# A hybrid block on one core: the first group's two batches as units of their own up to the first expert layer

## The chip, the core and the metric

One core of a Trainium2 chip runs the whole block as one program. Its engines are TensorE (PE, and PEld for its weight loads), VectorE (DVE), ScalarE (ACT), GpSimd (POOL) and the DMA queues, of which SP, ACT and POOL issue here. The metric is the device time of one execution in microseconds; lower is better.

## What is computed

The input is 8 batches of 256 tokens with 128 features, float32. Four layers follow one another, each on a layer-normalised input and added back to it: a state space layer, an expert layer, an attention layer, and the same expert layer again.

```python
x = x + state_space(layernorm(x))
x = x + experts(layernorm(x))
x = x + attention(layernorm(x))
x = x + experts(layernorm(x))
```

The state space layer normalises again, projects to a hidden part and a gate part of 256 channels each, runs a causal convolution of 4 taps and silu over the hidden part, derives from it delta (256 channels, through softplus) and the rows B and C (16 each), and then runs a recurrence over the tokens for every channel and each of 16 states:

```python
new = exp(A * d_t) * state + d_t * B_t * h_t
y = sum_n(new * C_t) + D * h_t      # then times silu(gate), then the output projection
```

The expert layer has 8 experts of width 352. A router gives each token its two best experts and their shares; every expert is computed for every token (gate, up, down) and weighted with its share, which is zero for all but two. Attention uses squared relu instead of softmax, and multiplies by u.

## The kernel before

The 8 batches are worked on as four groups of two, so a tile is 128 channels by 512 tokens. A group goes through these pieces, each a Python generator that gives out one operation at a time:

- `prelude` (s): statistics and row normalisation, transposition to channels by tokens, the hidden projection (`hid`), the convolution (for group 0 on DVE, L561 and L563; for groups 1 and 2 on PE, `conv`), the projection `xpj`, from which the B and C rows go to DRAM (`bc`, L585), and `dt` with softplus on ACT and DVE (L596 to L633), which gives `dl` (delta) and `du` (delta times h).
- `feeder`: loads the B and C rows of some states, spread over all partitions (`bt`, `ct`, L682, issued by SP), and computes the decays exp(A delta) on ACT (L697). There are three decay tiles in rotation.
- `recurrence` (m): on DVE, for each chunk of states and each of two channel halves, three instructions of 128x1024: multiply by `bt` (L744), scan (L749), multiply by `ct` (L753). A tile of 1024 holds 2 states of 2 batches. There are 16 such triples per group. All but some of the results are added up by accumulating DMAs that POOL issues (`adder`, L716).
- `gating` (g): the gate projection and silu. `ending` (f): for groups 0 and 1 PE sums the states of the last tiles by multiplying with the identity (`y`), and DVE multiplies with the gate (L797). `tail` (t): the output projection and its addition to x (`pb_m`, L512).
- `rest` (r): `led_in` (layer norm, transposition `tp_p`, the router's logits `lg_p`, ranks and shares on DVE, L895 to L921, and the first expert's weighting, L940), `moe` (22 slices of gate `gp_p`, up `up_p`, down `dn_p`, with silu on ACT, L960, and the product `it_p` on DVE, L1000), attention, a second `led_in`, and a second `moe` (tiles ending in `_r`).

`led_in`, the end of `moe` and attention already know parts of a group (`PARTS`): a group in `SPLIT` has one part per batch. `SPLIT` is empty before, so every group is one part.

The order on the engines is made while the program is built. `Board` keeps for each engine the time at which it comes free in a plan, with a cost for each operation (`mm`, `act_us`, `dve_us`). At each step it asks every lane for its next operation, takes the earliest possible start, and among the lanes of that engine that can start then, the lowest rank (`RANKS`, one number for each piece and group; `feeder` and `adder` have one each). Where ACT has to change its function table, the plan adds 1.3 us to the operation, and to the comparison only where the operation became possible less than `LONG` ago. Where PE would be idle before an operation that begins a new PSUM tile, the plan fills the gap with matmuls of the identity by itself into that tile, one for each 0.23 us (`Board.do`; the matmul stands at L325). The fillers are ordinary instructions of PE's list.

```python
            idle = t - max([self.free.get(op.engine, 0.0)] + [h.used for h in op.out])
            for _ in range(int((idle - 0.3) / self.FILL)):
                op.fill()
```

Of the kernel before, what the change touches and what calls it, by code (L numbers as in the profile page):

```python
# [31 lines left out]
class Board:  # L32
# [4 lines left out]
    PATIENCE, LONG = 0, 0  # L37
# [58 lines left out]
def kernel(  # L96
# [27 lines left out]
    nc = tc.nc  # L124
# [26 lines left out]
        "s": [0, 4, 4, 1.5], "m": [1.5, 2, 3, 3.5],  # L151
        "g": [4, 0, 3.5, 2], "t": [0, 3.5, 3.5, 0.5],
        "r": [2, 0.5, 2.5, 0.5], "f": [2.5, 1.5, 4, 0.5], "w": [0, 0, 0.3, 0], "feeder": 5, "adder": 0,
    }
    SOON = ("p0", "p1", "r0", "p3", "r3")
    SPLIT = ()
# [125 lines left out]
    def ring(pool, shape, tag, name, bufs=1):  # L282

        held = rings.setdefault((pool.name, tag), [])
        free = held[-bufs].used if len(held) >= bufs else 0.0
        h = Held(pool.tile(shape, FP, tag=tag, name=name, bufs=bufs), free)
        held.append(h)
        return h
# [91 lines left out]
    ]  # L380
    xh = [
# [4 lines left out]
    padding = [Held(t) for t in padded]  # L386
# [131 lines left out]
    def prelude(g):  # L518

        GB = SIZES[g]  # L520
        G = GB * T
        xn = yield from layernorm(Held(xs[g]), f"m{g}", "m", rms=True, parts=xh[g])
        for held in xh[g]:
            yield from biased(held, b_first)
        xT = ring(norm, [P, G], "xTm", f"xT_m{g}")
        yield from transposed(xn, f"m{g}", xT, scale=col("norm_scale"))

        h = [ring(mam, [P, G], f"h{c}", f"h_{g}_{c}", bufs=2) for c in range(NI)]  # L530
        cv = ring(mam, [P, NI, GB, T], "ex", f"cv_{g}")
        for c in range(NI):
            hp = padding[c]
            ps = bank([P, G], f"hid_{g}_{c}")
            yield pe(mm(G), [ps], [xT], product(ps.ap, [(in_w_sb[:, c * P : (c + 1) * P], xT.ap)]))
            yield act(act_us(G), [hp], [ps], lambda: nc.scalar.activation(
                hp.ap[:, 0:GB, K - 1 :], ps.ap.rearrange("p (b t) -> p b t", b=GB),
                AF.Identity, bias=col("in_b", c),
            ))
            shut(ps)  # L540

            if g in CONV:
                cps = bank([P, GB, T], f"conv_{g}_{c}")
                yield pe(K * mm(G), [cps], [hp], product(
                    cps.ap, [(taps_sb[:, k, c, :], hp.ap[:, 0:GB, k : k + T]) for k in range(K)]
                ))
                yield act(act_us(G), [h[c]], [cps], lambda: nc.scalar.activation(
                    h[c].ap.rearrange("p (b t) -> p b t", b=GB), cps.ap, AF.Silu,
                    bias=col("conv_b", c),
                ), SILU)  # L550
                shut(cps)
                continue

            if g > 0:
                yield act(act_us(G), [cv], [hp], lambda: nc.scalar.mul(
                    cv.ap[:, c], hp.ap[:, 0:GB, 0:T], col("conv_w", c)
                ))

            def taps():
                if g == 0:  # L560
                    nc.vector.tensor_scalar_mul(cv.ap[:, c], hp.ap[:, 0:GB, 0:T], col("conv_w", c))  # L561
                for k in range(1, K):
                    nc.vector.scalar_tensor_tensor(  # L563
                        cv.ap[:, c], hp.ap[:, 0:GB, k : k + T], col("conv_w", k * NI + c),
                        cv.ap[:, c], ALU.mult, ALU.add,
                    )

            yield dve((K - (g > 0)) * dve_us(G), [cv], [hp], taps)
        for c in range(0 if g in CONV else NI):
            yield act(act_us(G), [h[c]], [cv], lambda: nc.scalar.activation(  # L570
                h[c].ap, cv.ap[:, c].rearrange("p b t -> p (b t)"), AF.Silu, bias=col("conv_b", c)
            ), SILU)


        ps = bank([P, G], f"xpj_{g}")
# [4 lines left out]
        ww = ring(mam, [P, NI, G], "ww", f"ww_{g}")  # L580
# [3 lines left out]
        bc = Held(dram.tile([2 * N, G], FP, tag="bc", name=f"bc_{g}"))  # L584
# [4 lines left out]
        dl = [ring(mam, [P, G], f"dl{c}", f"dl_{g}_{c}", bufs=2) for c in range(NI)]  # L589
        ex = ring(mam, [P, NI, G], "ex", f"ex_{g}")  # L590
        for c in range(NI):
            ps = bank([P, G], f"dt_{g}_{c}")
# [19 lines left out]
        du = [ring(mam, [P, G], f"du{c}", f"du_{g}_{c}", bufs=2) for c in range(NI)]  # L612
# [29 lines left out]
        led_up[g] = bc, h, xT, dl, du  # L642

    def gating(g):

        xT = led_up[g][2]
        G = SIZES[g] * T
        gate = [ring(mam, [P, G], f"g{c}", f"g_{g}_{c}") for c in range(NI)]
        for c in range(NI):
            ps = bank([P, G], f"gat_{g}_{c}")  # L650
            w0 = I + c * P
            yield pe(mm(G), [ps], [xT], product(ps.ap, [(in_w_sb[:, w0 : w0 + P], xT.ap)]))
            yield act(act_us(G), [gate[c]], [ps], lambda: nc.scalar.activation(
                gate[c].ap, ps.ap, AF.Silu, bias=col("in_b", NI + c)
            ), SILU)
            shut(ps)
        gates[g] = gate
# [8 lines left out]
    def feeder():  # L666

        for g in range(NG):
            while f"s{g}" not in done:
                yield None  # L670
            GB = SIZES[g]
            G = GB * T
            NC = CHUNK // GB
            bc, h, _, delta, du = led_up[g]
            for q in range(N // NC):
# [4 lines left out]
                for tag, r0 in (("bt", q * NC), ("ct", N + q * NC)):  # L680
                    t = ring(scan, [P, NC, G], tag, f"{tag}_{g}_{q}", bufs=2)
# [5 lines left out]
                fed[g, q] = *rows_at, das  # L687
                for c in range(NI):
# [15 lines left out]
                    yield act(0.81 * NC, [da], [delta[c]], issue, EXP)  # L704
# [4 lines left out]
    def adder():  # L709

        while len(done & {f"f{g}" for g in range(NG)}) < NG:
# [3 lines left out]
            g, us, acc, st, into, of = sums.pop(0)  # L715
# [4 lines left out]
            landed[g] = landed.get(g, 0) + 1  # L720
# [3 lines left out]
    def recurrence(g):  # L724
        GB = SIZES[g]
# [3 lines left out]
        bc, h, _, delta, du = led_up[g]  # L729
# [4 lines left out]
        for q in range(NQ):  # L734
            for c in range(NI):
                while not spare():
                    yield None
                st = state([P, NC, G], f"st_{g}_{q}_{c}")
                if q == 0:
                    acc.append(st)  # L740
                while len(fed.get((g, q), [[]])[-1]) <= c:
                    yield None
                bt, ct, das = fed[g, q]
# [13 lines left out]
                elif q > 0:  # L757
                    sums.append((g, 6.3, acc[c], st, acc[c].ap, st.ap))
                    count[c] += 1
                elif g > 0:  # L760

                    sums.append((g, 4.5, acc[c], h[c], acc[c].ap[:, 0, :], h[c].ap))
                    count[c] += 1
        recurred[g] = acc, last, sum(count)
# [5 lines left out]
    def ending(g):  # L770

        G = SIZES[g] * T
        NC = CHUNK // SIZES[g]
        acc, last, count = recurred.pop(g)
        bc, h, _, delta, du = led_up[g]
        if g in FOLD:
            for c in range(NI):
                sums.append((g, 4.5, acc[c], acc[c], acc[c].ap[:, 0, :], acc[c].ap[:, 1, :]))
                count += 1
        while landed.get(g, 0) < count or g not in gates:  # L780
            yield None
        for c in range(NI):
            if g in FOLD:
                yield dve(dve_us(G), [du[c]], [gates[g][c], acc[c]], lambda: nc.vector.tensor_mul(
                    du[c].ap, acc[c].ap[:, 0, :], gates[g][c].ap
# [3 lines left out]
            y = bank([P, G], f"y_{g}_{c}")  # L789
# [7 lines left out]
            yield dve(dve_us(G), [du[c]], [gates[g][c], y], lambda: nc.vector.tensor_mul(  # L797
                du[c].ap, y.ap, gates[g][c].ap
# [3 lines left out]
    def tail(g):  # L802
        gates.pop(g)
        bc, h, _, delta, du = led_up.pop(g)
        G = SIZES[g] * T
        yield from forked((RANKS["t"][g], g), [
            project_back(
                xh[g][p], of_part(g, p, du), out_w_sb, f"m{g}{p}"
            ) for p in range(len(PARTS[g]))
        ])  # L810
# [407 lines left out]
    def rest(g):  # L1218
# [15 lines left out]
        yield from forked((RANKS["r"][g], g), [led_in(g, "p", key, p, first) for p in parts])  # L1234
# [5 lines left out]
    for g in range(NG):  # L1240
        waiting.append(Lane((RANKS["s"][g], g), prelude(g), [f"g{g - 1}"] * (g > 0) + [f"t{g - 2}"] * (g > 1)))
        waiting[-1].name = f"s{g}"
        waiting.append(Lane((RANKS["m"][g], g), recurrence(g), [f"s{g}"] + [f"m{g - 1}"] * (g > 0)))
        waiting[-1].name = f"m{g}"
        waiting.append(Lane((RANKS["g"][g], g), gating(g), [f"s{g}"] + [f"t{g - 1}"] * (g > 0)))
        waiting[-1].name = f"g{g}"
        waiting.append(Lane((RANKS["f"][g], g), ending(g), [f"m{g}"]))
        waiting[-1].name = f"f{g}"
        waiting[-1].patience = RANKS["w"][g]
        waiting.append(Lane((RANKS["t"][g], g), tail(g), [f"f{g}", f"g{g}"] + [f"t{g - 1}"] * (g > 0)))  # L1250
        waiting[-1].name = f"t{g}"
        waiting.append(Lane((RANKS["r"][g], g), rest(g), [f"t{g}"] + [f"r{g - 2}"] * (g > 1)))
        waiting[-1].name = f"r{g}"
# [57 lines left out]
```

## Time and profile before

Three runs gave 758.62, 758.63 and 759.3 us, median 758.63. The profiled execution took 758.34 us.

| What | Value |
|---|---|
| profiled execution | 758.34 us |
| its span (first to last instruction) | 756.6 us |
| granted PE clock, mean | 0.999 |
| DVE, recurrence: multiply, scan, multiply | 1.23, 2.31, 1.22 us each, 64 of each |
| first multiply of the recurrence on DVE | at 39.66 us |
| first expert layer, first gate matmul | at 153.44 us |
| table loads on ACT | 89 of 1.28 us, and one at the start |
| DMA, mean | 117 GB/s |

How to read such a page: part 1 gives each engine's busy time, its share of the span and its instructions. A matmul of this kernel is recorded as two halves, so 428 recorded fillers are 214 matmuls. The chain that ended last follows from the last instruction back to what released it; its shares say which engine set the end. A row of the groups has line, engine, operation, the tile written and the tiles read, shape, count, then busy time, mean of one in ns, and the idle time before it with what ended most of it. Names are without their numbers: `y` stands for all tiles of that name. In the window tables the first columns are the window, its length, then PE, PEld, DVE, ACT and POOL busy with the count of instructions, the granted clock, the DMA share and GB/s.

### The profile page before, as it was taken

The numbers are of one execution on the slowest core, as the hardware profiler recorded it, in microseconds if no ns is written. First come the engines' busy times: TensorE is split into PE (matmuls) and PEld (weight loads), VectorE is DVE, ScalarE is ACT, GpSimd is POOL, SyncE is SP. The second block draws the span as 40 slices with busy tenths as digits, with TensorE's granted clock in tenths as the row PEclk, the third lists the DMA queues.
The fourth block names the chain that finished last, engine by engine and source line by source line (L and its number), as shares of the span: only waits on it lengthen the run. The fifth ranks groups of instructions, "written<-read, shape, count | busy, mean of one in ns | idle before, by whom it ended". The sixth has DMA issues, their size and how long they took to land.

```text
span 756.6 us, 8464 instructions
## 1 busy us (share of the span) xinstructions
PE 737.7 (98%) x3093; PEld 403.6 (53%) x3093; DVE 568.6 (75%) x824; ACT 431.1 (57%) x570; POOL 89.8 (12%) x110
## 2 busy tenths in 40 slices
PE   4999999999999999999999999999999999999997
PEld 3877996853446744434754533443555434644343
DVE  2599999999999999899999998995735334354332
ACT  5578333799947879977876677742252322432220
POOL 2021110311112210002120110011100001000000
PEclk9999999999999999999999999999999999999999
DMA  8719795399763345655774666745011200000110
GB/s 260 209 57 220 169 219 162 98 228 218 166 171 84 76 124 133 166 133 138 176 170 96 159 161 179 160 102 109 2 42 27 72 15 14 15 29 29 47 36 14
DMA packets 38903, 88.63 MB, mean 117 GB/s; under 512 B 4339, under 2 KB 14542, under 8 KB 38862
## 3 DMA queue, kind: packets, MB, share of 16 engines
q0 software_dynamic: 9312, 30.94, 22.8%
q1 hardware_dynamic: 20624, 41.54, 17.2%
q10 hardware_dynamic: 8926, 15.61, 6.8%
q8 instruction: 24, 0.39, 0.2%
q14 instruction: 17, 0.14, 0.0%
HBM read 55.71 MB, written 1.44 MB: 76 GB/s over the span
## 4 chain that ended last, share of the span: by engine, by line
PE 78%; DVE 15%; ACT 3%; issue 2%; ACTq 0%; DVEq 0%
PE gp_r L487 10%; PE dn_r L1006 10%; PE dn_p L1006 9%; PE gp_p L487 9%; PE up_r L986 7%; PE up_p L986 7%; DVE st L749 6%; PE up_r L993 3%; DVE st L744 3%; PE up_p L993 3%; DVE st L753 2%; PE av_a L1197 2%; PE tp_p L325 1%; PE xpj L325 1%; PE v_a L1131 1%
## 5 line engine op out<-in xcount | busy, mean ns | idle before, releaser
L749 DVE TENSOR_TENSOR_SCAN st<-decay,st 128x1024 f32<-128x1024 f32 x64 | 147.8, 2309 | 2.5
L960 ACT ACTIVATE sg_r<-gp_r,zero 128x512 f32<-128x512 f32 x88 | 59.9, 687 | 109.8 <-PE gp_r L487 88.7
L57 ACT ACT_TABLE_LOAD x89 | 114.2, 1283 | 8.0 <-PE dn_r L1006 3.6
L697 ACT ACTIVATE decay<-dl,zero,a_sb 128x510 f32<-128x510 f32 x128 | 96.2, 804 | 36.9 <-DVE st L749 35.7
L1000 DVE TENSOR_TENSOR it_r<-up_r,sg_r 128x512 f32<-128x512 f32 x88 | 60.4, 687 | 66.7 <-PE up_r L986 42.3
L960 ACT ACTIVATE sg_p<-gp_p,zero 128x512 f32<-128x512 f32 x88 | 59.3, 685 | 62.5 <-PE gp_p L487 46.6
L1000 DVE TENSOR_TENSOR it_p<-up_p,sg_p 128x512 f32<-128x512 f32 x88 | 60.3, 686 | 43.4 <-PE up_p L986 29.4
L1006 PE MATMUL dn_p<-it_p,wd_sb 128*128 128x512 f32 x176 | 91.2, 605 | 0.6 <-DVE it_p L1000 0.6
L1006 PE MATMUL dn_r<-it_r,wd_sb 128*128 128x512 f32 x176 | 90.5, 603 | 0.0
L716 POOL DMA_DIRECT2D st<-st x58 | 50.4, 874 | 334.2 <-DVE st L753 303.7
L487 PE MATMUL gp_r<-xT_r,wg_sb 128*128 128x512 f32 x176 | 90.0, 597 | 0.0
L487 PE MATMUL gp_p<-xT_p,wg_sb 128*128 128x512 f32 x176 | 89.0, 594 | 0.0
L744 DVE TENSOR_TENSOR st<-bt,du 128x1024 f32<-128x1024 f32 x64 | 78.8, 1231 | 0.0
L753 DVE TENSOR_TENSOR st<-st,ct 128x1024 f32<-128x1024 f32 x64 | 78.1, 1221 | 0.7
L986 PE MATMUL up_p<-wb_p,wu_sb 128*128 128x512 f32 x128 | 65.1, 594 | 0.0
L986 PE MATMUL up_r<-wb_r,wu_sb 128*128 128x512 f32 x128 | 64.9, 592 | 0.0
L1006 PEld LDWEIGHTS dn_p<-it_p,wd_sb 128*128 128x128 f32 x176 | 31.3, 189 | 47.1 <-issue 36.3
L487 PEld LDWEIGHTS gp_r<-xT_r,wg_sb 128*128 128x128 f32 x176 | 32.6, 190 | 42.7 <-issue 37.4
L1006 PEld LDWEIGHTS dn_r<-it_r,wd_sb 128*128 128x128 f32 x176 | 31.6, 190 | 44.3 <-issue 39.5
L487 PEld LDWEIGHTS gp_p<-xT_p,wg_sb 128*128 128x128 f32 x176 | 32.8, 190 | 41.2 <-issue 36.3
L325 PEld LDWEIGHTS y<-ident 128*128 128x128 f32 x428 | 48.0, 192 | 1.2 <-PE dt L487 0.8
L325 PE MATMUL y<-ident 128*128 128x128 f32 x428 | 48.2, 275 | 0.0
(217 smaller groups left out, 853.1 us busy)
## 6 DMA issues: line engine op xcount, KB each, us to landing
st<-st POOLq DMA_DIRECT2D x54, 512.0 KB, 6.4
bt<-bc SPq DMA_DIRECT2D x32, 512.0 KB, 6.0
ct<-bc SPq DMA_DIRECT2D x32, 512.0 KB, 4.5
wb_r<-wrow_r ACTq DMA_DIRECT2D x30, 256.0 KB, 3.8
wb_p<-wrow_p ACTq DMA_DIRECT2D x29, 256.0 KB, 3.9
st<-h POOLq DMA_DIRECT2D x6, 256.0 KB, 4.9
wg_sb<-in_L_ffn_w_gate_dram SPq DMA_DIRECT2D x2, 704.0 KB, 4.7
wu_sb<-in_L_ffn_w_up_dram SPq DMA_DIRECT2D x2, 704.0 KB
```

The source lines that it names most:

```text
L57: self.load_tables(op.table)
L325: nc.tensor.matmul(ps[:, 0:n], lhsT=ident[:, 0:m], rhs=ident[:, 0:n], start=True, stop=True)
L487: nc.tensor.matmul(ps, lhsT=lhsT, rhs=rhs, start=(i == 0), stop=(i == len(terms) - 1))
L697: nc.scalar.activation(shaped[:, n, :, 1:], delta[c].ap.rearrange("p (b t) -> p b t", b=GB)[:, :, 1:], AF.Exp, bias=zero, scale=a_sb[:, c, ...
L716: yield load(us, [acc], [st], lambda: nc.gpsimd.dma_start(into, of, accum_op=ALU.add), "POOL", 0.9)
L744: yield dve(1.22, [st], [bt, du[c]], lambda: nc.vector.tensor_mul(st.ap, bt.ap, du[c].ap.unsqueeze(1).to_broadcast([P, NC, G])))
L749: yield dve(2.29, [st], [das[c]], lambda: nc.vector.tensor_tensor_scan(flat, das[c].ap.rearrange("p n t -> p (n t)"), flat, 0.0, ALU.mult, ...
L753: yield dve(1.22, [st], [ct], lambda: nc.vector.tensor_mul(st.ap, st.ap, ct.ap))
L960: yield act(act_us(G), [sg], [gp], lambda: nc.scalar.activation(sg.ap, gp.ap, AF.Silu, bias=zero), SILU)
L986: nc.tensor.matmul(ps.ap, lhsT=wu_sb[:, i * P : (i + 1) * P], rhs=wa.ap[:, cols_of], start=True, stop=True,)
L1000: yield dve(dve_us(width), [it], [ps, sg], lambda: nc.vector.tensor_mul(it.ap, ps.ap, sg.ap[:, cols_of]))
L1006: yield pe(mm(dn.ap.shape[1]), [dn], [it], lambda: nc.tensor.matmul(dn.ap, lhsT=wd_sb[:, i, :], rhs=it.ap[:, cols_of], start=(i == 0), sto ...
```

## The change

Group 0 is put into `SPLIT`, and its two batches become units (`UNITS`). Every piece of the state space layer now runs per unit: `prelude`, `gating`, `feeder`, `recurrence`, `ending` and `tail` take a unit. Groups 1 to 3 are one unit each, as before. The units of a group share their tiles: `room` gives each unit its half of the group's tile and keeps the halves' use times apart. A unit of one batch has 4 states in a tile of 1024 rather than 2 states of 2 batches, so it has 8 triples; both together have 16, as before. A decay tile then takes 4 activations of 128x255 where it took 2 of 128x510.

`rest(0)` starts after the first unit's `tail`. The second batch's `led_in` waits until its own unit's `tail` is done. Before the expert layer the two parts are joined to one again, so `moe`, attention and what follows work on 512 tokens as before.

Besides, some ranks differ (`s` of group 0, `m` of group 3, `g` of group 3, `f` of group 2, and `feeder`), and `LONG` is 1.4 in place of 0.

```diff
-    PATIENCE, LONG = 0, 0
+    PATIENCE, LONG = 0, 1.4
...
-        "s": [0, 4, 4, 1.5], "m": [1.5, 2, 3, 3.5],
-        "g": [4, 0, 3.5, 2], "t": [0, 3.5, 3.5, 0.5],
-        "r": [2, 0.5, 2.5, 0.5], "f": [2.5, 1.5, 4, 0.5], "w": [0, 0, 0.3, 0], "feeder": 5, "adder": 0,
+        "s": [1.5, 4, 4, 1.5], "m": [1.5, 2, 3, 2.5],
+        "g": [4, 0, 3.5, 0.5], "t": [0, 3.5, 3.5, 0.5],
+        "r": [2, 0.5, 2.5, 0.5], "f": [2.5, 1.5, 3.5, 0.5], "w": [0, 0, 0.3, 0], "late": 0, "feeder": 2.5, "adder": 0,
...
-    SPLIT = ()
+    SPLIT = (0,)
...
+    def room(pool, u, tag, name, both=False, bufs=1):
+
+        g, lo, hi = UNITS[u]
+        if (g, tag, name) not in rooms:
+            shape = [P, NI, SIZES[g] * T] if both else [P, SIZES[g] * T]
+            rooms[g, tag, name] = ring(pool, shape, tag, f"{name}_{g}", bufs)
+            rooms[g, tag, name].views = []
+        t = rooms[g, tag, name]
+        ap = t.ap[:, :, lo * T : hi * T] if both else t.ap[:, lo * T : hi * T]
+        h = Held(ap, t.used)
+        t.views.append(h)
+        return h
...
+    UNITS = [(g, lo, hi) for g in range(NG) for lo, hi in PARTS[g]]
+    UNITS_OF = [[u for u, unit in enumerate(UNITS) if unit[0] == g] for g in range(NG)]
...
-        bc = Held(dram.tile([2 * N, G], FP, tag="bc", name=f"bc_{g}"))
+        bc = Held(dram.tile([2 * N, G], FP, tag=f"bc{lo}{g in SPLIT}", name=f"bc_{u}"))
...
-                    yield act(0.81 * NC, [da], [delta[c]], issue, EXP)
+                    yield act((0.35 + 0.0009 * G) * NC, [da], [delta[c]], issue, EXP)
...
-        yield from forked((RANKS["r"][g], g), [led_in(g, "p", key, p, first) for p in parts])
+        def come(p):
+            while f"t{UNITS_OF[g][p]}" not in done:
+                yield None
+            yield from led_in(g, "p", key, p, first)
+
+        yield from forked((RANKS["r"][g], g), [come(p) for p in parts])
+        if len(parts) > 1:
+
+            joined = Held(xs[g])
+            joined.ready = max(h.ready for h in xh[g])
+            joined.used = max(h.used for h in xh[g])
+            PARTS[g][:], xh[g][:] = [(0, SIZES[g])], [joined]
...
+    for u, (g, lo, hi) in enumerate(UNITS):
+        prior = [v for v in UNITS_OF[g - 1]] if g > 0 else []
+        older = [v for v in UNITS_OF[g - 2]] if g > 1 else []
+        lane("s", u, g, prelude(u), [f"g{v}" for v in prior] + [f"t{v}" for v in older])
+        lane("m", u, g, recurrence(u), [f"s{u}"] + [f"m{u - 1}"] * (u > 0))
+        lane("g", u, g, gating(u), [f"s{u}"] + [f"t{v}" for v in prior])
+        lane("f", u, g, ending(u), [f"m{u}"])
+        lane("t", u, g, tail(u), [f"f{u}", f"g{u}"] + [f"t{u - 1}"] * (u > 0))
+        if lo == 0:
+            lane("r", g, g, rest(g), [f"t{u}"] + [f"r{g - 2}"] * (g > 1))
```

## The prediction

> **What bounds the kernel now.** I read the page first (engine shares, then the chain that ended last), then the chain in order of time, then the busy time by stage, and last the instructions of ACT and DVE in the opening.
>
> ```profile
> PE 737.7 (98%) x3093; PEld 403.6 (53%) x3093; DVE 568.6 (75%) x824; ACT 431.1 (57%) x570; POOL 89.8 (12%) x110
> ...
> PE 78%; DVE 15%; ACT 3%; issue 2%; ACTq 0%; DVEq 0%
> ...
> L697 ACT ACTIVATE decay<-dl,zero,a_sb 128x510 f32<-128x510 f32 x128 | 96.2, 804 | 36.9 <-DVE st L749 35.7
> ...
> L325 PE MATMUL y<-ident 128*128 128x128 f32 x428 | 48.2, 275 | 0.0
> ```
>
> PE's 98% is not all work. The last row is the planner's filler: 428 recorded halves are 214 matmuls of the identity by itself, 48.2 us, 0.225 us each. The list of PE's instructions holds 564 such fillers, some 127 us. DVE holds 15% of the chain, and the chain in order of time says where:
>
> ```profile
> 43.53 1.54 ACT xn_m L437 x4
> 45.79 3.18 DVE st L749
> ...
> 126.97 1.13 DVE st L744
> 128.76 1.83 PE pb_m L506 x14
> ...
> 193.66 2.29 DVE st L749
> 197.13 1.14 DVE st L753
> ```
>
> From 45.79 to 128 us the chain is DVE alone: the first group's state space recurrence, 16 triples (multiply, scan, multiply) at 4.79 us each. Then comes the lead-in of the first expert layer; its first gate matmul starts at 153.44 in PE's timeline. DVE carries the chain again in parts until 198; from there to the end the chain is PE. The stages:
>
> ```profile
> 0.00:40.00 40.00, 29.10 (x191) 23.63 (x192) 16.67 (x47) 22.83 (x38) 5.47 (x25) 1.00 0.76 222
> ...
> 80.00:120.00 40.00, 39.95 (x333) 37.60 (x332) 39.05 (x28) 13.46 (x18) 6.07 (x7) 1.00 0.83 198
> 120.00:153.00 33.00, 32.48 (x208) 25.24 (x207) 32.31 (x54) 19.77 (x26) 7.74 (x7) 1.00 0.43 119
> 153.00:200.00 47.00, 46.42 (x157) 20.99 (x154) 46.42 (x43) 44.53 (x52) 6.88 (x8) 1.00 0.84 203
> 200.00:500.00 300.00, 299.33 (x1102) 148.22 (x1103) 279.35 (x393) 226.30 (x284) 43.86 (x45) 1.00 0.59 143
> ```
>
> [...] DVE is full from 40 to 200 us. After that PE has 0.67 us of idle in 300, so a microsecond won or lost before 200 us reaches the end if PE's stream stays whole.
>
> **The change part by part.** Everything is made against the profiled execution, 758.34 us (span 756.6 and 1.74 around it); the median of the three runs is 758.63, 0.3 above.
>
> *PE's own ledger.* PE runs its list in order, fillers too, so I compare the lists of both programs.
> - Fillers: 564 before, 519 after; 45 x 0.225 = 10.1 us removed. Of them 35 (7.9 us) stand ahead of the first gate matmul, 10 (2.3 us) behind it.
> - Sums over the states: a unit of one batch holds 4 states per tile, where the group held 2. So the 10 matmuls of 128x512 become 36 of 128x256. In PE's timeline a 512 gate matmul steps by 0.86 us and four 256-wide av_a matmuls take 1.73, so 0.433 each: 36 x 0.433 - 10 x 0.86 = +7.0 us, all ahead of the gate.
> - The eight products of 512 that the group's hid, xpj, dt and gat steps need become sixteen of 256: 16 x 0.433 - 8 x 0.86 = 0.
> - One hid product of the third group moves from ahead of the gate to behind it: 0.86 each way.
>
> Ahead of the gate: -7.9 + 7.0 - 0.9 = -1.8 us. Behind it: -2.3 + 0.9 = -1.4 us. Together -3.1 us if PE's idle time stays as it is.
>
> *DVE and ACT in the opening.* ACT normalises both batches before it makes the 10 skip and tap tiles (about 3 us). Before, three of the four xn tiles stood behind them and the first copy of the transposed rows ran at 12.94; now the first half can run at about 12.4 and takes 0.4, not 0.69. Every step to the first scan is half as long and the second unit's runs beside it. A half DVE step is taken at 0.36 us, between half of the 0.69 row and the 0.415 of uT, which is 128x256. Step by step this puts the second triple's end at about 43 us, where it was 50.2. Of these 7 us, 1.8 go back: the next group's row statistics stood ahead of the first multiply and now stand behind the fourth scan. Split work costs DVE more small steps before the router's shares are ready: two sets of seven ranking steps (1.9 us each, estimated between the 0.19 row of 32 elements and the 0.42 of 256, against 2.37 for one whole set, +1.4), two sets of shares and differences (+1.0), halved gating products, adds and guards (+0.5), and the first unit's weighting product, now ahead (+0.4): +3.3. So the router's shares are ready -7 + 1.8 + 3.3 = -1.9 us earlier, 147.3 where it was 149.2. The gate then follows after the transposition of the shares and the convolution of the third group, which now stands wholly ahead of it: about 152.4 by this path, 151.6 by PE's ledger. PE reaches the first expert layer's last product some 2 to 3 us earlier by either. DVE's list from shares to the last it_p of that layer is the same but for 0.3 us (12 scans, 25 products of 1024, 32 of 512), so DVE neither returns nor adds anything there.
>
> *Decays, where a rule speaks against it.* A decay tile was two ACTIVATEs of 128x510 (804 ns each, two in 1.52 us) and is now four of 128x255. No row has that shape with these operands. Bounds: half of the row, 1.5 us a tile (no change), and the whole row again, 3.0 us (+1.5). The Trainium skill, "ScalarE: Activation LUTs", section "What ACT_TABLE_LOAD costs", gives an ACTIVATE a fixed 186 ns, 93 ns for each pointer operand (here bias and scale), 0.833 ns an element, and lets neighbours overlap by 93 ns. That makes 797 ns at 510, which the row's 804 bears out, and so four take 4 x 584 - 3 x 93 = 2.06 us, an estimate: +0.54 a tile, 8.6 us over 16. By the rule taken alone the split costs 8.6 us; by the trace it costs nothing while ACT waits for the scan:
>
> ```profile
> 96.61 1.52 ACT L697 ACTIVATE decay<-dl,zero,a_sb 128x510 f32<-128x510 f32 x2 [3.21 <-DVE st L749]
> ```
>
> There are 3.2 us of cover in each triple, and three decay tiles in rotation. I take +0. If the cover were gone, it would be 0.54 a triple. The cover is thinnest from 43 to 90 us, where ACT also does the gates and the next group's preparation.
>
> *DMA and queues.* SP now issues two writes of the B and C rows (32 KB each) and the second stands ahead of the first load of unit 0. It waits for the second unit's copy on ACT, about 0.9 us after the first. Before, the write went out at 26.51 and the load at 28.19; behind it land bt loads in 6.4 us. Now I expect the load at 24 to 25, landing at 31, when DVE's first multiply wants it (31 to 32). DMA is full with weights until 24 (1.17 in the window 22 to 24, 0.42 after), so it can't be much earlier, and the cost is 0 to 1.5 us; I take 0. The number of bt and ct loads and their size stay. On POOL 12 accumulating adds become 8; the last pair of each unit goes to PE, so POOL's queue gets shorter, and nothing waits there. ACT's list has 86 table loads, before 90.
>
> *Ranks and LONG* move work of later groups. Behind the first expert layer the lists hold 103 fillers before and 102 after, and the same products. The second expert layer of group 0 starts later in PE's list and the third group's state space work ends some 15 us of PE work sooner. The cover is DVE's idle time, 20.7 us of the 300 from 200 to 500, which the third group's sooner end takes up in part; if it is gone, PE waits. I take 0, between -1 and +3.
>
> Sum: -3.1 us by PE's ledger, -2 to -3 by DVE; I take -2.8: **755.5 us**.
>
> **The rivals.**
> - *A larger gain*: the opening's 7 us less 1.8 and only 1.4 of DVE's extra steps show, and the layer starts 4 us sooner, with 1.4 behind: 753. Against it: fillers are instructions. PE can't be sooner than its ledger, unless idle falls too, and from 40 to 153 only 1.7 us of it are left. So the floor is near 753.
> - *The gain doesn't reach the end*: the later groups' new order gives 2 to 3 us of PE waits on it_p or it_r, which get no fillers, since their sums are open; then 758. For it: DVE is at 93% from 200 to 500. Against it: now 1.97 us of such idle stand between 153 and 700.
> - *Slower: ACT's decays fall behind the scan.* Place: 43 to 90 us, ten triples. ACT needs ten decay tiles at 2.06 (20.6), eight table loads at 1.28 (10.3) and 7.6 us of preparation: 38.5 us of 47.9. From 9.4 us of blocked time in that stretch on it sets the pace (ACT runs in order, and the silu steps between the decays wait for PE's convolutions, behind fillers). At 5.2 us a triple 14 triples cost +5.7, and -2.8 becomes +3: 761.5.
> - *The change does nothing* because the second unit still ends the wait: the expert layer needs both batches, and no gate matmul stands ahead of the second unit's lead-in. That is so, and it is why the gain is 3 us and not the 38 (eight triples) that lie between the units' ends. It is in the likeliest case already.
>
> **How the numbers follow.** Likeliest 0.52 (754 to 757), larger gain 0.10 (752.5 to 754), gain lost on the way 0.20 (757 to 760), slower 0.18 (760 to 764). Only changes above 0.2% (1.5 us) can be told from none here: faster is below 757.1, slower above 760.1. Faster 0.60, within 0.22, slower 0.18. The range leaves out the lowest twentieth and most of the slow case: 752.8 to 760.6.
>
> **What would show it.** Right: the second scan's multiply ends near 43 us; the first gate matmul starts at 151 to 153; fillers of y, tp_m and we_p take some 8 us less; PE's busy time is near 734.6 and its idle near 19; the chain is DVE from 34 to 135. Wrong: waits of DVE's scan on ACT's decay between 45 and 90 (slower case); a DMA wait of the first multiply over 1.5 us; PE waits on it_p or it_r above 2 us from 200 to 500; a first gate before 150 (larger gain). I would be wrong above all if the chip runs later than the plan behind the gate, where PE gets no fillers to show it.

## The result

The changed kernel takes 760.85 us (median of 13 runs, 760.11 to 761.66), the kernel before 759.42 (13 runs, 758.62 to 760.02). The ratio is 1.0021, 95% interval 1.0014 to 1.0029: 1.4 us slower, where 2.8 us faster was forecast. The profiled execution took 761.44 us (span 759.4). That pair of profiles shows 3.1 us, more than the medians do: 758.34 lies below all 13 runs of before, 761.44 near the top of those after. The traces of the experiments serve as further records of both openings below.

Lines of the page after, in the order of those of before (busy time, shares of the chain, decays), and the rows of PE's fillers for `y` and of the new decay shape from the groups by shape:

```profile
PE 738.6 (97%) x3071; PEld 407.2 (54%) x3071; DVE 572.9 (75%) x861; ACT 438.8 (58%) x616; POOL 92.0 (12%) x109
...
PE 73%; DVE 18%; DMA 3%; ACT 2%; issue 2%; POOL 0%; ACTq 0%; DVEq 0%; POOLq 0%
...
L725 ACT ACTIVATE decay<-dl,zero,a_sb 128x510 f32<-128x510 f32 (+1 forms) x160 | 105.1, 717 | 18.2 <-DVE st L778 17.8
```

```profile
L343 PE MATMUL y<-ident 128*128 128x128 f32 x152 | 17.5, 275 | 0.0
```

```profile
L725 ACT ACTIVATE decay<-dl,zero,a_sb 128x255 f32<-128x255 f32 x64 | 32.9, 588 | 8.1 <-DVE st L778 8.0
```

The fillers of `y` fell from 48.2 to 17.5 us, but PE's busy time rose by 0.9 and its idle time from 18.9 to 20.8. DVE's part of the chain grew, and DMA is in it for the first time. The stages (window, length, PE, PEld, DVE, ACT, POOL busy, clock, DMA; those of before stand in the prediction):

```profile
0.00:40.00 40.00, 29.67 (x196) 26.56 (x197) 21.63 (x59) 26.88 (x59) 5.87 (x26) 1.00 0.72 222
80.00:120.00 40.00, 39.86 (x312) 36.67 (x311) 39.38 (x51) 26.25 (x40) 5.09 (x5) 1.00 0.55 134
120.00:153.00 33.00, 31.34 (x215) 27.31 (x214) 32.35 (x49) 18.41 (x27) 7.41 (x7) 1.00 0.51 133
153.00:200.00 47.00, 46.23 (x152) 20.73 (x151) 45.91 (x40) 44.03 (x53) 6.88 (x8) 1.00 0.91 213
200.00:500.00 300.00, 297.14 (x1085) 144.88 (x1084) 276.47 (x391) 218.27 (x276) 47.76 (x45) 1.00 0.58 140
```

DVE does 5 us more by 40 us: the opening did get tighter. From 200 to 500 PE, which had 0.67 us of idle, has 2.86. So something was won early and lost later.

The chain in order of time shows what the opening hangs on. Before:

```profile
14.18 2.15 PE hid L487 x4
16.34 7.82 PE xpj L325 x70
24.15 1.72 PE xpj L487 x4
```

After:

```profile
12.67 3.78 PE hid L510 x8
16.45 6.49 PE xpj L343 x52
22.94 1.73 PE xpj L510 x8
```

In both, the projection `xpj` waits for neither the taps on DVE nor the silu on ACT, but for its own fillers, 35 before and 26 after, which stand ahead of it in PE's list. The margin is not the same: the last silu of the group ends at 22.60 before, 1.4 us ahead of the first product of `xpj`, and at 22.38 after, 0.4 ahead. The prediction built its opening step by step from DVE's taps and missed this row of before.

### The profile page after: what moved, and what is told of

Its sections match the earlier page's. It is cut to its first block, busy times and chain, and to the rows that moved or that the text cites. A ratio compares the mean times of both kernels' runs of the same rounds, so it can differ in the third digit from the quotient of the medians.

```text
span 759.4 us, 8493 instructions
## 1 busy us (share of the span) xinstructions
PE 738.6 (97%) x3071; PEld 407.2 (54%) x3071; DVE 572.9 (75%) x861; ACT 438.8 (58%) x616; POOL 92.0 (12%) x109
## 4 chain that ended last, share of the span: by engine, by line
PE 73%; DVE 18%; DMA 3%; ACT 2%; issue 2%; POOL 0%; ACTq 0%; DVEq 0%; POOLq 0%
PE dn_r L1032 10%; PE dn_p L1032 10%; PE gp_r L510 9%; PE gp_p L510 9%; DVE st L778 7%; PE up_r L1012 7%; PE up_p L1012 7%; DVE st L773 4%; DVE st L782 3%; PE up_r L1019 3%; PE up_p L1019 3%; DMA wb_r<-wrow_r 2%; PE av_a L1223 2%; PE v_a L1157 1%; PE pb_a L529 1%
## 5 line engine op out<-in xcount | busy, mean ns | idle before, releaser
L725 ACT ACTIVATE decay<-dl,zero,a_sb 128x510 f32<-128x510 f32 (+1 forms) x160 | 105.1, 717 | 18.2 <-DVE st L778 17.8
L744 POOL DMA_DIRECT2D st<-st x54 | 47.0, 882 | 321.8 <-DVE st L782 285.7
L1012 PEld LDWEIGHTS up_r<-wb_r,wu_sb 128*128 128x128 f32 x128 | 23.5, 190 | 29.5 <-issue 25.9
L1012 PEld LDWEIGHTS up_p<-wb_p,wu_sb 128*128 128x128 f32 x128 | 23.8, 190 | 28.7 <-issue 27.6
```

Source lines behind the costliest of these rows:

```text
L725: nc.scalar.activation(shaped[:, n, :, 1:], delta[c].ap.rearrange("p (b t) -> p b t", b=GB)[:, :, 1:], AF.Exp, bias=zero, scale=a_sb[:, c, ...
L744: yield load(us, [acc], [st], lambda: nc.gpsimd.dma_start(into, of, accum_op=ALU.add), "POOL", 0.9)
L1012: nc.tensor.matmul(ps.ap, lhsT=wu_sb[:, i * P : (i + 1) * P], rhs=wa.ap[:, cols_of], start=True, stop=True,)
```

## The experiments

Times are medians; the ratio is to the kernel before, run on the same chip, with its 95% interval.

**Which part of the edit acts.** First the two halves of the change by themselves: the split with `RANKS` and `LONG` of before, and the other way round, `SPLIT = ()` with the new ranks and `LONG`.

> The split with the ranks and LONG of before. Theory A (the new order of the later groups is what costs the 2.9 us behind the first expert layer; the split by itself gains): 757 to 759, below the kernel before. Theory B (the split needs the new ranks: with the old ones PE's list holds 574 fillers, 161 of them behind the first gate matmul against 124 in the changed kernel, 37 x 0.225 = 8.3 us more): 766 to 770.

> The new ranks and LONG without the split (SPLIT empty). Theory A (the order of the later groups costs 2.9 us whatever the opening does): 762 to 763. Theory B (the ranks were made for the split; PE's list holds 587 fillers against 564, 24 more behind the first gate, 5.4 us): 764 to 766. If the split alone is the loss: 759, as before.

Measured: 769.83 us (1.0139, 1.0125 to 1.0153) and 770.93 us (1.0153, 1.0139 to 1.0167). Each half alone costs 10 to 12 us; together they cost 1.4. So the split can't be judged apart from the ranks, and "Ranks and LONG: I take 0" was no small term. With the old ranks the router's shares of the first group come at 154.1, 131.5 us after `xpj`, where the changed kernel needs 125.3.

Then the late ranks alone were put back (`m` and `g` of the last group, `f` of the third):

```diff
-        ... "m": [1.5, 2, 3, 2.5],
-        "g": [4, 0, 3.5, 0.5], ... "f": [2.5, 1.5, 3.5, 0.5], ...
+        ... "m": [1.5, 2, 3, 3.5],
+        "g": [4, 0, 3.5, 2], ... "f": [2.5, 1.5, 4, 0.5], ...
```

> The split with the new ranks of the opening (s of group 0, feeder) and LONG, but the old ranks of m and g of group 3 and f of group 2. Theory A: the waits of the later groups go, 757.5 to 759. Theory B (11 more fillers behind the first gate matmul than in the changed kernel, 2.5 us): 762.5 to 764.

Measured: 761.11 us (1.0021, 1.0011 to 1.0031), as the changed kernel. Both expectations missed. In sum the late ranks neither won nor lost anything. In the trace two things offset each other behind the first layer: 11 fillers more, and shorter waits of PE (by 1.3 us).

**Is a filler's time the end's time?** `FILL` from 0.23 to 0.30, all else in the same order:

> The changed kernel with FILL at 0.30 where it is 0.23: same plan and the same order of everything else, only each gap of the plan is given fewer filling transposes. Theory A, the prediction's ledger (TensorE is busy almost throughout, so a filler that is gone is 0.225 us gone from the end): some 124 fillers fewer give -28 us, about 733 us. Theory B (nearly every filler lies in a gap that something else sets, so its going leaves idle time in its place, and the ledger's count of fillers was no forecast of the end): within 2 us of the changed kernel, 759 to 762.5, with TensorE's idle time up by about 26 us.

Measured: 759.47 us (1.0004, 0.9994 to 1.0015), 1.4 below the changed kernel and not 28. Theory A falls as a rule for the whole kernel: 126 fillers, 28 us of PE's list, went, and 17 us more of idle time and slower matmuls took their place. PE's clock fell to 0.94 from 40 to 160 us. The time is theory B's, but its 26 us of idle were 17, and the clock had no place in it.

**The half-speed start.** After, the eight halves of `hid` took 3.78 us; in the same place before, four of twice the width took 2.36. Putting fillers ahead (`board.free["PE"]` 4.0 in place of 9.0) warms PE:

> The changed kernel with the plan's first free time of TensorE at 4 us where it is 9: all other engines keep their order, TensorE gets 13 fillers ahead of the first transpose and 3 more before the first projection, which ran at half speed (a pair of 128x256 halves took 0.85 us, later ones 0.43). Theory A (the half-speed start, some 2 us of TensorE time, is what took the opening's gain): the first projections at 0.43 to 0.5 us a pair, router's shares and first gate matmul 1 to 2 us earlier, 758.5 to 760. Theory B (the opening goes by VectorE's chain and the half-speed matmuls reach the end for little, or the fillers delay the first transpose): gate within 0.7 us, 760.3 to 761.5.

Measured: 759.99 us (1.0009, 1.0001 to 1.0017), 0.9 below the changed kernel, with 16 more fillers. The row of `hid` in PE's timeline, of the changed kernel and then of this one:

```profile
12.67 3.78 PE L510 MATMUL hid<-xT_m,in_w_sb 128*128 128x256 f32 x8 [2.38 <-ACT xT_m L480]
```

```profile
14.23 2.29 PE L510 MATMUL hid<-xT_m,in_w_sb 128*128 128x256 f32 x8
```

It starts 1.6 us later, since the transposes now stand behind fillers, and is done at the same 16.5. What is won comes behind it: the 26 fillers of `xpj` run in 5.97 us and not in 6.70. Gate and layer's end come 0.6 us sooner. The time lies in theory A's range, the shift of the gate in theory B's: the warm start is worth well under 1 us here, where A had 1 to 2.

**The convolution ahead of the gate.** From shares to first gate matmul the changed kernel takes 6.0 us, before 4.2, because the third group's convolution (`conv`, 3.4 us) now stands wholly between them, where 1.1 us of it ran ahead of the shares; its fillers and a wait of 0.22 us come on top. Held back until four gate matmuls are out:

```diff
             if g in CONV:
+                while g == 2 and not begun:
+                    yield None
```

> The changed kernel, with the third group's first convolution held until the first four gate matmuls of the first expert layer have been issued; the order around it is otherwise the same. Theory A (the convolution, 3.4 us of TensorE between router's shares and first gate, ate the opening's gain, which then reaches the end): first gate near 152.3, first expert layer's last down product 1.5 to 2 us earlier than 230.0, 758.8 to 759.7. Theory B (the convolution is only moved within a stretch that TensorE fills; or VectorE's work of the third group, now later, sets the attention's start behind the first layer): gate near 152.3, last down product of the first layer within 0.7 us, 760.3 to 762.

> The early fillers and the later convolution together. If both losses are what they seem and add up, 757 to 759, the prediction's gain; if neither reaches the end, 760.3 to 762; if they are worth something alone and nothing together, the same wait stands behind both.

Measured: 762.47 us (1.0033, 1.0021 to 1.0045), above both theories, and with the warm start 761.46 (1.0030, 1.0020 to 1.0040), where neither reached the end. The gate came at 149.37, 4.8 us sooner, and the layer's end at 232.7, 2.7 later. PE's timeline and the window behind it show why:

```profile
165.03 1.94 PE L1022 MATMUL up_p<-wb_p,wu_sb 128*32 128x512 f32 x8 [3.48 <-ACT h L577]
163.00:171.00 8.00, 5.97 (x17) 2.52 (x18) 7.92 (x8) 7.91 (x10) 1.01 (x2) 0.57 1.03 244
```

An up product waits 3.48 us for ACT's silu of the convolution, presumably for the PSUM bank that the convolution still holds, and from 163 to 171 us the clock falls to 0.57. In the changed kernel the same wait is 0.72 and the clock there 1.00. So the 1.8 us between shares and gate are real, but moving the convolution doesn't win them.

**Late fillers.** None behind the first gate matmuls (`board.FILL = 1e9` from there on), in the changed kernel, in the one before, and with the warm start:

> The changed kernel without any filling transposes behind the first gate matmuls (118 fewer, 26 us of TensorE time); the order of all else stays. Theory A (behind the first layer the plan's gaps have closed by the time the chip comes to them, because VectorE and the loads of the token weights run late there, so fillers that were planned into gaps delay real work; that is the 2.9 us lost between 230 us and the end): 757.5 to 759.5, last down product 1.5 to 3 us earlier. Theory B (they lie in true gaps): within 0.7 us of the changed kernel, 760.2 to 761.5, with some 26 us more of TensorE idle time. A third outcome: TensorE's clock falls in the idle stretches, and it is slower than 762.

> The same for the kernel before: no filling transposes behind its first gate matmuls (133 fewer). Theory A (the changed kernel lost its gain to fillers that its own plan misplaced): nothing to win here, 758.8 to 760. Theory B (late fillers delay both kernels alike): 756 to 758, so that the changed kernel's arrears of 1.4 us stay.

> The changed kernel with the early fillers of the warm start and none behind the gate. If both act by themselves the gains add up: the warm start was worth 0.9 us, so 0.9 us below the changed kernel without late fillers; a better kernel than both if that comes below 758.5.

Measured: 766.15 us (1.0089, 1.0056 to 1.0122), 762.98 (1.0046, 1.0029 to 1.0063) and 769.14 (1.0131, 1.0117 to 1.0145): the third outcome of the first, in all three; the other two expectations had no place for it. The clock column fell where the attention stands behind the first layer; the changed kernel without late fillers, by stage:

```profile
200.00:230.00 30.00, 30.00 (x87) 11.88 (x86) 28.09 (x32) 17.27 (x20) 3.44 (x4) 1.00 0.73 175
230.00:260.00 30.00, 24.60 (x58) 11.71 (x57) 24.40 (x52) 14.88 (x21) 9.97 (x6) 0.67 0.25 60
```

With its fillers the changed kernel has this in the second window:

```profile
230.00:260.00 30.00, 29.68 (x162) 21.70 (x161) 28.05 (x64) 24.16 (x36) 11.23 (x7) 1.00 0.22 54
```

Without them PE has 5.4 us of idle, a clock of 0.67, and the first `u_a` (the attention's first projection) comes 8.5 us later. A filler costs up to 0.225 us where PE is late, and its absence costs more where the clock falls for it.

A milder cut, 0.30 behind the gate only (32 fewer with the warm start in the changed kernel, 33 fewer in the one before):

> The changed kernel with the early fillers of the warm start, and FILL at 0.30 behind the first gate matmuls only (30 late fillers fewer). Where all were thinned to 0.30, 2.2 us came back behind the first expert layer; where all late ones were gone the clock fell to 0.66. Theory A (the late fillers are slightly too many and those that are left keep the clock): 757.3 to 758.8, both gains together. Theory B (what came back there came from the thinner filling ahead of the gate, or thinning by itself is worth nothing): 759.5 to 760.5, as with the warm start alone.

> The kernel before with FILL at 0.30 behind its first gate matmuls only (33 late fillers fewer). Theory A (only the changed kernel's plan has drifted from the chip behind the first layer, so only there do late fillers delay work): 759 to 760, no gain. Theory B (the plan has too many late fillers in both): 757 to 758.3, so that the changed kernel's arrears behind the first layer are not the fillers' doing.

> The kernel before with 21 fillers ahead of its first transposes (TensorE free at 4 us in the plan) and FILL at 0.30 behind the gate. If the warm start is worth in it what it was in the changed kernel (0.9 us), 757.3 to 758; its first projections ran 2.36 us where 1.7 is full speed, so 0.6 is the likely bound, and if the fillers delay the transposes by as much, 758.3 to 759.

Measured: 758.89 us (0.9991, 0.9983 to 1.0000) and 758.42 (0.9989, 0.9981 to 0.9998). By the medians thinning is worth about 1 us in both (1.1 and 0.9), so the late fillers aren't what set the changed kernel back. The single traces are less even: behind the layer they show 1.5 and 0.5. The warm start put upon the latter gave 759.72 (1.0006, 0.9998 to 1.0015), above both ranges expected: in that kernel it lost 1.3 us. None of these beats the kernel before by more than the 0.2% that can be told.

**`LONG`.** Back to 0 behind the gate in the changed kernel, and 1.4 alone in the kernel before:

> The changed kernel with LONG back at 0 from the first gate matmuls on: the plan then has 180 late fillers where it has 118, and six more table loads. Theory A (LONG is what makes the plan behind the split good; its going costs what the plan shows, 62 fillers or up to 14 us, as part of the 10 us that the split with the old ranks lost): 768 to 775. Theory B (LONG costs 2.9 us behind the first layer): 757.5 to 759.

> The kernel before with LONG at 1.4 alone: six table loads fewer, 10 late fillers more. Theory A (LONG alone is worth nothing, it is needed only with the split): 759 to 762. Theory B (it costs some 3 us behind the first layer in any kernel): 762 to 764.

Measured: 771.51 us (1.0150, 1.0135 to 1.0164) and 765.26 (1.0072, 1.0059 to 1.0086). Theory A holds for the first and B, even more than forecast, for the second: alone `LONG` costs 5.9 us, 3.8 of it behind the first layer, yet taking it out of the split plan costs 10.7. The same number is good or bad by the plan it falls into. The 3.8 us are not the loss of the changed kernel: in the trace of k1 they go with 14 fillers more behind the layer and a stretch of low clock,

```profile
258.00:262.00 4.00, 4.00 (x7) 1.73 (x6) 3.86 (x9) 2.40 (x5) 0.65 (x1) 0.57 0.70 132
```

and the changed kernel has neither: one filler less than before there, and a clock of 1.00.

**Does a gain in the opening reach the end?** Two of the four taps of group 0 are left out, with plan and order unchanged, in both kernels. Then, in the changed one, 14 fillers of the opening are left out as well:

```diff
-                for k in range(1, K):
+                for k in range(1, K) if g > 0 else (1,):
...
-            for _ in range(int((idle - 0.3) / self.FILL)):
+            for _ in range(int((idle - 0.3) / (self.FILL if t > 25 else 0.47))):
```

> The changed kernel, leaving out two of the four taps of the first group's convolution (8 half-size steps of 0.48 us on VectorE, 3.8 us, all on the opening's chain; the output is then not the reference's); plan and order are the same. Theory A (what is won in the opening reaches the end): shares 3 to 3.8 us earlier, 757 to 758. Theory B (the first expert layer is full on TensorE and VectorE to its end at 230 us and gives an earlier opening back): shares 3 us earlier, the layer's end less than 1 us earlier, 760 to 761.5.

> The kernel before, leaving out the same two taps of the first group (4 full-size steps of 0.75 us, 3.0 us; the output is then not the reference's). Theory A: 756 to 757. Theory B: 758.5 to 760.

> d1 (two taps of the first group left out, so the output is not the reference's), and besides 14 of the 29 filling transposes ahead of and around the first state projection gone (13 ahead of it where 26 stood), 3.2 us of TensorE's stream. Theory A (up to the gate the time is TensorE's stream, fillers included; the chip cannot run ahead of the plan): first state projection near 19.5 us where it was 22.5, first gate 2.5 to 3.3 us earlier, 757.5 to 758.7. Theory B (a gain at the gate is given back in the first expert layer or behind it): gate earlier as in A, 760 to 761.5.

Measured: 760.92 us (1.0021, 1.0014 to 1.0028), 759.40 (1.0001, 0.9992 to 1.0009) and 757.77 (0.9980, 0.9971 to 0.9990). Without the taps, 3.8 and 3.0 us of DVE's chain, neither kernel moves: even the earlier shares that both theories of d1 expected didn't come. With the 14 fillers gone as well, 3.15 us come off the median, which is 14 x 0.225, but the match is in part luck: in the traces it is 2.0 at the gate and at the layer's end, and 2.4 in the span. The chains of the two, without the taps and then without the fillers too:

```profile
13.03 3.78 PE hid L510 x8
16.81 5.81 PE xpj L343 x52
22.62 1.73 PE xpj L510 x8
```

```profile
12.88 3.78 PE hid L510 x8
16.66 3.92 PE xpj L343 x26
20.58 1.73 PE xpj L510 x8
```

The taps ended 3.1 us sooner without moving `xpj` by more than 0.3. This settles what bounds the opening up to `xpj`: PE's list, fillers included. And what is won there passes through: in d2 `xpj`, shares, gate and layer's end are each 2.0 us sooner than in d1. Fillers alone, with all taps kept, were thinned only in f1: six fewer ahead of `xpj`, which came 0.7 us sooner.

## Why the prediction was wrong

Set side by side, the traces fall into four lengths that hardly vary within a plan (start of the first `xpj` product on PE, last step of the shares on DVE, first gate matmul, last down product of the first expert layer, end of the span; us):

| Kernel | xpj starts | to shares | to gate | to layer's end | to end |
|---|---|---|---|---|---|
| before | 23.99 | 125.23 | 4.22 | 76.70 | 526.5 |
| before, fewer taps (d0) | 25.16 | 125.25 | 4.21 | 76.70 | 526.3 |
| before, trimmed (h0) | 25.07 | 125.22 | 4.22 | 76.66 | 525.9 |
| after | 22.77 | 125.35 | 6.01 | 75.89 | 529.4 |
| after, late ranks old (e3) | 23.31 | 125.34 | 6.00 | 75.89 | 529.4 |
| after, warm start (p1) | 22.16 | 125.33 | 6.01 | 75.89 | 528.9 |
| after, fewer taps (d1) | 22.46 | 125.33 | 6.00 | 75.90 | 528.7 |
| after, fewer taps and fillers (d2) | 20.42 | 125.34 | 6.01 | 75.89 | 528.3 |

The three plans of before are one and the same up to the gate but for d0's taps; `hid` took 2.36 us in the first record and 3.47 and 3.30 in the others, so `xpj` in the profiled execution was early by about 1.1 (the two further records with this opening have 24.6, k1, and 25.2, g0). Against the other two (25.1) the change sums to -2.3 + 0.1 + 1.8 - 0.8 + 2.7 = +1.5 us, where the medians differ by 1.43. (The last term is the mean of 529.4, 529.4, 528.9 and 528.7 less that of 526.5 and 526.3; h0 is left out because its late fillers are thinner, d2 because of its opening. With the mean of all records of either opening the first term is -1.9 and the sum +1.9, so it holds to about half a microsecond.)

- *Opening, "-7 + 1.8 + 3.3 = -1.9"*: shares were ready at 148.12, 1.1 to 2.3 us sooner than in the records of before. The size was right by luck, for the reason was wrong. The second triple ended at 45.3 and not near 43, and 3.8 of these 4.9 us were given back up to the shares, where 5.1 of 7 were counted. So from `xpj` to the shares both kernels take the same 125.3 us: what the split wins at the first triples its small steps give back, and the equality is chance. All that was won stands ahead of `xpj`: nine fillers fewer (-2.0) and a `hid` that starts 1.3 us sooner, less slower matmuls (`hid` +0.3 against 3.47, the 26 fillers 6.70 us where 5.85 was due, +0.8). Half-size taps took 1.83 us for a set of four where 1.45 was assumed, and that cost nothing, as d1 shows.
- *PE's ledger, "-1.8 ahead of the gate"*: the rule that PE can't be sooner than its list held in the opening (d1, d0, d2). Terms were missing: the half speed of the start (`hid` counted at no difference, and up to +1.4 against the profiled record of before) and, in PE's recorded busy time, products that were halved without being counted (skip +0.4, shares +0.3, `tp_p` +0.2). As a rule for the whole kernel it was wrong: between opening and gate, and behind it, DVE and ACT set most gaps (f1), and fillers keep the clock (g1, pg1).
- *Shares to gate, 5.1 us counted*: 6.0 measured, 4.2 before. Of the gain at the shares at most 0.5 us was left at the gate (154.13, against 153.44 to 154.62), and against the profiled record of before it came 0.7 later.
- *"DVE neither returns nor adds anything" in the first layer*: it was 0.8 us shorter (75.9 for 76.7), so the layer ended 0.1 to 1.3 us sooner, where 2 to 3 were forecast.
- *"Ranks and LONG ... I take 0, between -1 and +3"*: this is the step that turned the sign. From the layer's end on the changed plan takes 2.7 us longer. The sum was off by 4.2 us (-2.8 forecast, +1.4 measured); the other 1.5 is the gain that the layer's end lacked. The range named the size; the number of fillers behind (103 and 102, "and the same products") was taken for evidence that the time would be the same, and it isn't. The ledger's own -1.4 behind the gate fails with it.
- *Decays, bt load, POOL*: as forecast but for small shifts. Four decays of 128x255 took 2.07 us, the 2.06 that was worked out from the Trainium skill, "ScalarE: Activation LUTs", section "What ACT_TABLE_LOAD costs", and the scan waited 0.5 us in all for a decay (the third rival didn't come). The first load of `bt` was issued at 25.8 us, where 24 to 25 was forecast, and the first multiply had no DMA wait.

Where do these 2.7 us lie? PE's waits from 230 to 740 us, before:

```profile
PE base_a L487 <- ACT xT_a L457: 0.5, 1, 0.5
PE ot_r L476 <- ACT oT_r L468: 0.3, 1, 0.3
PE we_p L933 <- DVE we_p L921: 0.2, 1, 0.2
PE ot_p L476 <- ACT oT_p L468: 0.2, 1, 0.2
```

and after:

```profile
PE dn_r L1032 <- DVE it_r L1026: 1.0, 1, 1.0
PE up_r L1012 <- DVE wb_r L1003: 0.8, 1, 0.8
PE gp_r L510 <- DVE it_p L1026: 0.6, 1, 0.6
PE tp_a L475 <- DVE xn_a L445: 0.2, 1, 0.2
```

Unrounded, the sums are 1.1 and 2.6: 1.5 us more. Two of the three large waits, 1.6 us, are for `it_r` and `it_p`, the tiles that the second rival named; its sign of being wrong was 2 us. The third is for the token weights (`wb_r`), and the wait for `it_p` comes 7 us after DVE itself had stood 5.15 us for them. DVE's waits from 300 to 500 us, before and after:

```profile
DVE wb_r L977 <- DMA wb_r<-wrow_r: 1.2, 2, 1.1
```

```profile
DVE wb_r L1003 <- DMA wb_r<-wrow_r: 8.1, 3, 5.2
```

The load behind the longest of these was issued at 317.35 us, within a microsecond of two others of its kind, and took 8.9 us to land; the median of such loads is 4.6 after and 3.8 before.

The rest is no wait that the profile names. In the two profiled executions the stretch is 2.9 us longer: 1.3 of idle time and 1.6 of busy time. Taken from the start of one matmul record to the start of the next, the four waits account for 1.5 us, and delays of 0.05 to 0.3 us between matmuls, each too short to be listed as a wait, for another 1.6. No matmul is slower. All of it is lost before about 560 us, where the third group's attention has its first projection; from there on both kernels step alike. Which edit does it stays open: the late ranks change nothing in sum (e3), thinner fillers help both kernels by the medians alike (h1, h0), `LONG` alone costs by another way (k1) and can't be taken out of the split plan without a far worse one (l1). The opening's ranks (`s` of group 0, `feeder`) and the split's own shift of what follows were not separated. That the late load causes its part is read from the waits; no run takes it away alone.

## What to carry to other kernels

Where an engine's gaps are filled by counted instructions, look for the fillers in the chain of waits first: here a gain on another engine was worth nothing as long as fillers stood ahead of the consumer, and one that shortened the list as well reached the end. A count of fillers is not a forecast of time, for it says where a plan expected gaps, and the clock may need them. Ranks of a greedy planner are no small print: cost each half of such a change alone, and take the planner's later stages as open unless their waits were followed too.

## What the runs showed of the hardware

- PE ran at half speed until about 15 us in the profile of before, 17 to 18 in d0's and after, and 12 in the warm start, while the clock column said 1.00: in the changed kernel identity halves took 421 ns at 9.7 us and 275 later, and the 128x256 halves of `hid` 634 ns against 379 in the warm start. The Trainium skill, "TensorE: Matmul & The Clock Gate", Part 1, has the clock halved by default until some 3.4 us of steady work; with 5.1 us of fillers ahead (p1), whose halves turned from 421 to 275 ns 4.0 us after the first, `hid` ran at full speed, which agrees. It had a place in the prediction's ledger. The point of change moves from one execution to the next, which is where the 1.1 us between the records of before come from.
- Without fillers, and with single waits of PE of up to 3.5 us, the clock column fell to 0.67 over 30 us (g1); in the kernel before, with another order of the same pieces and no wait above 1.2 us, to 0.94 (g0). It can also fall where PE is busy throughout by its records: to 0.57 from 258 to 262 us in k1. Why is not shown.
- Half-size VectorE steps save less than half: a tap steps by about 0.48 us at 128x256 and 0.75 at 128x512.
